# Rotary squares added on GpSimd, and projections and norms one step earlier, in a windowed-attention kernel

## The chip, the cores and the metric

The kernel runs on one core of a Trainium2 chip. A core has five engines that run their own instruction streams: TensorE (PE, matrix multiplication; its weight loads are listed as PEld), VectorE (DVE), ScalarE (ACT), GpSimd (POOL) and SyncE (SP, which here only starts DMAs). They meet at semaphores. TensorE writes its results to PSUM[...]; VectorE and ScalarE read PSUM, GpSimd works on SBUF alone in this kernel. The metric is the device time of one execution in microseconds.

## The reference, cut to what matters

The input x has 2048 tokens of 128 features. The reference applies a six-layer local-attention transformer, then a linear-attention block, and then the six layers again with the same weights:

```python
x = x + 0.5 * _L0_ffn_ref(_layernorm(x), ...)     # six layers
x = x + _L0_attn_ref(_layernorm(x), ...)          # linear attention and an MLP
x = x + 0.5 * _L0_ffn_ref(_layernorm(x), ...)     # six layers again

# one of the six layers; 16 heads of 64, window 32
q, k, v = split(shift_tokens(x) @ Wqkv)
q = l2norm(q) * q_scale;  k = l2norm(k) * k_scale
q = q * cos * scale + rotate_half(q) * sin * scale
k = k * cos / scale + rotate_half(k) * sin / scale
sim = 8 * q @ k.T                                  # each 32-token window sees itself and the one before
x = softmax(masked sim) @ v @ Wo + x
x = gated_gelu_ffn(layernorm(shift_tokens(x))) + x # hidden width 341
```

The change concerns `l2norm`: the sum of squares of a head's 64 query or key features. The kernel holds the features of a head as two rotary halves of 32, so that a sum of squares has two parts.

## The kernel before, in words

Data are kept transposed, features on partitions and tokens along the row: xa is the stream between layers, xf the stream between attention and feed-forward. All arithmetic is fp32 except the mask.

`ffn_module(m, last)` runs the six layers; it is called twice, and `linear_module` stands between the calls. A layer is cut into NAC = 8 chunks c of AC = 256 tokens, and the feed-forward into NCH = 4 pieces f of CH = 512 tokens. The attention of a chunk has four steps, each for 128 tokens and half of the heads.

The parts that the change touches, for layer l and chunk c:

- `tables(l, s)` (L187): four GpSimd products that scale the rotary tables for queries (s = 0) or keys (s = 1), once a layer.
- `project(l, c, g)` (L203), g = 0 to 3: for queries and for keys two matmuls (L218) write the two halves of four heads into one PSUM bank each. `rotate(s)` (L222) multiplies the bank by the tables on VectorE (prod, L224) and adds the two products on GpSimd into abq or abk (L230). `square(s)` (L234) takes the bank's squares on ScalarE into a tile sq (L236) of 128 x 2 x 256: half, token. There are four sq tiles, two abq tiles and three abk tiles in turn.
- `square_sums(l, c, g2)` (L247): matmuls with 32 columns of a selection matrix sum the squares over the partitions of each head into the PSUM tile ss. Four column groups u take four sq tiles; the two halves are added by accumulation, so there are eight matmuls a call and two calls a chunk (L254).
- `norms_a` (L310) and `norms_b` (L321): a reciprocal square root with one Newton step. VectorE clamps ss (L314), ScalarE takes logarithm, exponential and square (L315, L316, L318), VectorE finishes rn in two instructions (L325, L326).
- `scale_keys(l, c, g2)` (L342): two matmuls r (L347) spread rn over the partitions, two VectorE products scale abk with it (L353), and `gather` (L293) then starts eight DMAs that bring the keys into head order, hk. `gather(l, c, "q", g2)` does the same for unscaled queries, hq; query norms go into the softmax's scale through `query_norms` (L328: matmuls nt, copy rq).

Around them stand `values_proj` (pv, L271, copied to v by ScalarE, L272), `values_windows` (three DMAs that lay out windows, ve and vo), `earlier_keys` (pk, L367), `similarities` (sim, L383 and L391, then maxima and their scaling on VectorE, L402 and L403), `exponentials` (eight of L417 a step on ScalarE), `normalised` (reciprocal L427, product on GpSimd L429), `transposed` (te, L443, copied to eT by VectorE, L444), `values` (av, L458, copied to oT by ScalarE, L464), `output` (y, L471, xf, L475) and `feed_forward` (a generator; mean, variance, broadcast, then three gates: matmuls pf (L513), a table load, the gelu gate (L518) and a table load back on ScalarE, then the product h (L522) on VectorE, and the output yf (L530, L534)).

The order of all this is written out by hand. `at(step, pos, fn, ...)` puts a call into a plan, and the plan is emitted by step and, in a step, by position; every engine then executes its instructions in that order. Step t0 = 32 l + 4 c is the first of chunk c's four steps of similarities, so each step holds a projection of a later chunk, the similarities of this one and the values of an earlier step. With four steps a chunk and eight a feed-forward piece the plan repeats every eight steps. Nothing but semaphores on data and on reused buffers holds the engines together. The PSUM tiles called small share five banks in turn, ss has one and sim has two; which earlier tile a new one replaces follows from the order of the calls.

The lines of the plan that the change touches, before it:

```python
at(t0 - 7 + g, 20, project, l, c, g)
at(t0 - 6 + 2 * g2, 45, square_sums, l, c, g2)
at(t0 - 3, 2, norms_a, l, c)
at(t0 - 3, 33, norms_b, l, c)
at(t0 - 3, 58, scale_keys, l, c, 0)
at(t0 - 2, 45, scale_keys, l, c, 1)
```

Of the kernel before, what the change touches and what calls it, by code (L numbers as in the profile page):

```python
# [10 lines left out]
ALU = mybir.AluOpType  # L11
# [29 lines left out]
def kernel(ctx: ExitStack, tc: tile.TileContext, a: dict, out: bass.AP):  # L41
    nc = tc.nc
# [19 lines left out]
    sel = const.tile([P, 3, 32], F32, name="sel")  # L62
# [63 lines left out]
    def ffn_module(m, last):  # L126
        with ExitStack() as st:
            wp = st.enter_context(tc.tile_pool(name=f"w{m}", bufs=1))

            def load_qk(l, g):  # L130
                w = wp.tile([P, 4, P], F32, tag=f"wqk{g}", name=f"wqk{g}_{m}_{l}")
                nc.sync.dma_start(w, a["Wqk"][l].rearrange("p (g f) -> p g f", g=4)[:, g, :]
                                  .rearrange("p (u f) -> p u f", u=4))
                return w
# [47 lines left out]
            def small(name):  # L182
                return ps_small.tile([P, CH], F32, tag="small", name=name)
# [14 lines left out]
            def chunk(l, c):  # L198
                if (l, c) not in chunks:
                    chunks[l, c] = {"nm": f"{m}_{l}_{c}"}  # L200
                return chunks[l, c]

            def project(l, c, g):  # L203

                d = chunk(l, c)
                nm = f"{d['nm']}_{g}"
                if g % 2 == 0:
                    for qk, bufs in (("q", 2), ("k", 3)):
                        d[qk, g // 2] = work.tile(
                            [P, 2, 2, AC], F32, tag=f"ab{qk}", name=f"ab{qk}_{nm}", bufs=bufs  # L210
                        )
                xs = xa[:, c * AC : (c + 1) * AC]
                both = []
                for s in range(2):
                    ps = small(f"p{s}_{nm}")
                    both.append(ps.rearrange("p (u t) -> p u t", u=2))
                    for u in range(2):
                        nc.tensor.matmul(  # L218
                            both[s][:, u, :], wqk[g][:, 2 * s + u, :], xs, start=True, stop=True
                        )  # L220

                def rotate(s):  # L222
                    prod = work.tile([P, 2, 2, AC], F32, tag="prod", name=f"prod{s}_{nm}", bufs=2)
                    nc.vector.tensor_tensor(  # L224
                        prod,
                        both[s].unsqueeze(2).to_broadcast([P, 2, 2, AC]),
                        tabs[l, s].rearrange("p (u v) t -> p u v t", u=2),
                        ALU.mult,
                    )
                    nc.gpsimd.tensor_tensor(  # L230
                        d["qk"[s], g // 2][:, :, g % 2, :], prod[:, 0], prod[:, 1], ALU.add
                    )

                def square(s):  # L234
                    sq = work.tile([P, 2, AC], F32, tag="sq", name=f"sq{s}_{nm}", bufs=4)
                    nc.scalar.activation(sq, both[s], AF.Square)  # L236
                    d["sq", g, s] = sq


                rotate(0)  # L240
                square(1)
                square(0)
                rotate(1)
                if c == NAC - 1 and l + 1 < DEPTH:
                    wqk[g] = load_qk(l + 1, g)

            def square_sums(l, c, g2):  # L247

                d = chunk(l, c)
                if g2 == 0:  # L250
                    d["ss"] = ps_ss.tile([P, 2, AC], F32, tag="ss", name=f"ss_{d['nm']}")
                for half in range(2):
                    for u in range(4):
                        nc.tensor.matmul(  # L254
                            d["ss"][32 * u : 32 * u + 32, 0, :],
                            sel[:, g2, :],
                            d["sq", 2 * g2 + u % 2, u // 2][:, half, :],
                            start=(g2 == 0 and half == 0), stop=(g2 == 1 and half == 1),
                        )

            def values_proj(l, c, i):

# [289 lines left out]
            def at(step, pos, fn, *args):  # L552
                plan.setdefault(step, []).append((pos, len(plan[step]) if step in plan else 0, fn, args))
# [5 lines left out]
            for l in range(DEPTH):  # L559
                for c in range(NAC):  # L560

                    t0 = per * l + STEPS * c
                    if c == 0:
                        at(t0 - 10, 46, tables, l, 0)
                        at(t0 - 8, 46, tables, l, 1)
                    for g in range(4):
                        at(t0 - 7 + g, 20, project, l, c, g)
                        at(t0 - 2 + g, 50, values_proj, l, c, g)
                    for g2 in range(2):
                        at(t0 - 6 + 2 * g2, 45, square_sums, l, c, g2)  # L570
                    for t in range(2):
                        at(t0 - 1 + 2 * t, 62, values_windows, l, c, t)
                    at(t0 - 5, 30, gather, l, c, "q", 0)
                    at(t0 - 3, 1, gather, l, c, "q", 1)
                    at(t0 - 3, 2, norms_a, l, c)
                    at(t0 - 3, 33, norms_b, l, c)
                    at(t0 - 3, 58, scale_keys, l, c, 0)
                    at(t0 - 2, 45, scale_keys, l, c, 1)
                    at(t0 - 2, 46, query_norms, l, c)
                    at(t0 - 1, 45, earlier_keys, l, c)  # L580
                    for s in range(STEPS):
                        at(t0 + s, 25, similarities, l, c, s)
                        at(t0 + s, 30, exponentials, l, c, s, 0)
                        at(t0 + s, 51, exponentials, l, c, s, 1)
                        at(t0 + s + 1, 3, normalised, l, c, s)
                        at(t0 + s + 2, 40, transposed, l, c, s, 0)
                        at(t0 + s + 2, 41, transposed, l, c, s, 1)
                        at(t0 + s + 2, 60, values, l, c, s)
                    for t in range(2):
                        at(t0 + 4 + 2 * t, 55, output, l, c, t)  # L590
                for f in range(NCH):
                    gen = feed_forward(l, f)
                    t0 = per * l + 8 * f
                    for step, pos in (
                        (11, 57), (12, 57), (13, 4), (13, 57),
                        (15, 57), (17, 57), (19, 57), (21, 57),
                    ):
                        at(t0 + step, pos, more, gen)
# [112 lines left out]
    def no_earlier():  # L711

        nc.gpsimd.memset(xa[64:P, 0:1], 0.0)

    ffn_module(0, False)
    linear_module()
    no_earlier()
    ffn_module(1, True)


# [103 lines left out]
```

## Time and profile before

| what | value |
|---|---|
| runs | 4289.59 us median of 3 (4288.85 to 4295.82) |
| the profiled execution | 4295.45 us, of which its span is 4293.6 us |
| granted TensorE clock, mean | 0.959 |
| squares, L236, ACT | 768 of 0.60 us, 435.6 us |
| sums of squares, L254, PE | 3072 records, 249.1 us |
| rotary adds, L230, POOL | 768 of 1.27 us, 974.7 us |
| norms on ACT, L315, L316, L318 | 96 each of 0.40, 0.37 and 0.38 us |
| norms on DVE, L314, L325, L326 | 96 each of 0.43, 0.41 and 0.42 us |
| key scaling, L353, DVE | 384 of 0.68 us |

An fp32 matmul appears as two records, so that 3072 records of L254 are 1536 matmuls. Matmuls are pipelined and the ends of their records are modelled: two records that follow each other overlap in the list, and the difference of their starts says what one costs. "[1.88 <-ACT gate L518]" behind an instruction says that its engine had been idle for 1.88 us before it, until line 518 on ACT released it. In a table of stages the clock's column is the granted share of TensorE's full clock.

### The profile page before, as it was taken

The numbers are of one execution on the slowest core, as the hardware profiler recorded it, in microseconds if no ns is written. First come the engines' busy times: TensorE is split into PE (matmuls) and PEld (weight loads), VectorE is DVE, ScalarE is ACT, GpSimd is POOL, SyncE is SP. The second block draws the span as 40 slices with busy tenths as digits, with TensorE's granted clock in tenths as the row PEclk, the third lists the DMA queues.
The fourth block names the chain that finished last, engine by engine and source line by source line (L and its number), as shares of the span: only waits on it lengthen the run. The fifth ranks groups of instructions, "written<-read, shape, count | busy, mean of one in ns | idle before, by whom it ended". The sixth has DMA issues, their size and how long they took to land.

```text
span 4293.6 us, 110203 instructions
## 1 busy us (share of the span) xinstructions
PE 3947.0 (92%) x41968; PEld 2744.5 (64%) x41968; DVE 2719.7 (63%) x5222; ACT 2846.8 (66%) x8784; POOL 1672.7 (39%) x1355
## 2 busy tenths in 40 slices
PE   7899999999999999999777899999999999999998
PEld 4666666666666666666445666666666666666665
DVE  4666666666676666665426566666666666766664
ACT  4676777767667676677225676767667676677766
POOL 4343444344344334332014344343343443443331
PEclk8999999999999999999788999999999999999998
DMA  3343433433334334342003343433434334343331
GB/s 105 86 107 89 101 100 94 103 94 101 97 92 112 93 95 110 87 102 68 8 25 91 85 109 89 104 98 96 101 95 107 93 96 106 87 109 97 91 99 49
DMA packets 323975, 393.67 MB, mean 92 GB/s; under 512 B 61052, under 2 KB 274808, under 8 KB 323448
## 3 DMA queue, kind: packets, MB, share of 16 engines
q1 hardware_dynamic: 323448, 386.61, 35.7%
q8 instruction: 334, 5.47, 0.5%
q14 instruction: 193, 1.58, 0.1%
HBM read 34.58 MB, written 1.05 MB: 8 GB/s over the span
## 4 chain that ended last, share of the span: by engine, by line
PE 23%; ACT 16%; DVE 7%; issue 2%; SPq 1%; DMA 1%; POOL 1%; ACTq 0%; DVEq 0%; POOLq 0%
ACT e L417 8%; PE p L218 5%; DVE prod L224 3%; PE y L471 2%; PE te L443 2%; ACT L516 2%; PE pv L271 2%; PE av L458 2%; PE sim L391 2%; PE ss L254 2%; SPq L305 1%; ACT v L272 1%; DVE sim L402 1%; ACT gate L518 1%; PE yf L530 1%
## 5 line engine op out<-in xcount | busy, mean ns | idle before, releaser
L417 ACT ACTIVATE e<-sim,st,rq 128x96 f32<-128x96 f32 x3072 | 1291.8, 440 | 570.9 <-DVE st L403 509.5
L429 POOL TENSOR_TENSOR e<-e,st 128x768 f32<-128x768 f32 x384 | 564.4, 1470 | 1869.1 <-DVE st L427 1540.3
L224 DVE TENSOR_TENSOR prod<-p,tab 128x1024 f32<-128x1024 f32 x768 | 918.6, 1211 | 235.5 <-ACT sq L236 129.4
L218 PE MATMUL p<-xa,wqk 128*128 128x256 f32 x3072 | 845.0, 420 | 120.4 <-ACT gate L518 115.4
L218 PEld LDWEIGHTS p<-xa,wqk 128*128 128x128 f32 x3072 | 592.0, 204 | 246.6 <-ACT gate L518 138.1
L236 ACT ACTIVATE sq<-p 128x512 f32<-128x512 f32 x768 | 435.6, 599 | 355.6 <-PE p L218 240.0
L417 ACT ACTIVATION_READ_ACCUMULATOR e<-sim,st,rq 128x1 f32 x3072 | 653.9, 213 | 0.0
L230 POOL TENSOR_TENSOR abq<-prod 128x512 f32<-128x512 f32 x384 | 489.0, 1273 | 188.2 <-DVE prod L224 144.4
L230 POOL TENSOR_TENSOR abk<-prod 128x512 f32<-128x512 f32 x384 | 485.7, 1265 | 72.5 <-DVE prod L224 63.7
L444 DVE COPY eT<-te 96x512 f32<-96x512 f32 x768 | 489.8, 677 | 3.6 <-PE te L443 3.6
L522 DVE SCALAR_TENSOR_TENSOR h<-pf,lvec,gate 128x512 f32<-128x512 f32 x144 | 107.9, 749 | 571.1 <-ACT gate L518 553.1
L471 PEld LDWEIGHTS y<-oT,wo 128*128 128x128 f32 x3072 | 374.4, 192 | 95.1 <-issue 49.5
L402 DVE TENSOR_REDUCE sim<-sim 128x4 f32<-128x384 f32 x768 | 426.5, 555 | 9.0 <-PE sim L391 8.8
L443 PE MATMUL te<-sq_consts,e 128*96 128x128 f32 x3072 | 424.1, 279 | 2.5 <-ACT gate L518 0.8
L271 PE MATMUL pv<-wv,xa 128*128 128x512 f32 x768 | 415.4, 623 | 10.6 <-DVE rstd L499 8.4
L458 PE MATMUL av<-eT,ve 96*64 96x64 f32 x6144 | 406.9, 229 | 4.6 <-DVE eT L444 4.5
L458 PEld LDWEIGHTS av<-eT,ve 96*64 96x64 f32 x6144 | 318.3, 138 | 132.5 <-issue 50.5
L272 ACT COPY v<-pv 128x512 f32<-128x512 f32 x384 | 227.6, 593 | 255.3 <-DMA ve<-v 171.1
L458 PE MATMUL av<-eT,vo 96*64 96x64 f32 x6144 | 385.8, 223 | 0.0
L471 PE MATMUL y<-oT,wo 128*128 128x128 f32 x3072 | 376.4, 276 | 4.5 <-ACT gate L518 3.0
L391 PEld LDWEIGHTS sim<-hk,hq 64*64 64x64 f32 x12288 | 279.1, 136 | 151.7 <-issue 136.4
L443 PEld LDWEIGHTS te<-sq_consts,e 128*96 128x96 f32 x3072 | 317.6, 127 | 59.5 <-DVE h L522 11.8
(141 smaller groups left out, 4954.9 us busy)
## 6 DMA issues: line engine op xcount, KB each, us to landing
hq<-abq SPq DMA_DIRECT2D x1536, 64.0 KB, 2.1
hk<-abk SPq DMA_DIRECT2D x1536, 64.0 KB, 2.1
vo<-v SPq DMA_DIRECT2D x192, 384.0 KB, 4.3
ve<-v SPq DMA_DIRECT2D x192, 256.0 KB, 3.5
ve<-v SPq DMA_DIRECT2D x180, 128.0 KB, 2.3
wqk<-in_Wqk SPq DMA_DIRECT2D x48, 256.0 KB, 3.6
wv<-in_Wv SPq DMA_DIRECT2D x24, 256.0 KB, 2.8
wo<-in_Wo SPq DMA_DIRECT2D x12, 512.0 KB, 5.0
```

The lines of the kernel that those rows point to most:

```text
L218: nc.tensor.matmul(both[s][:, u, :], wqk[g][:, 2 * s + u, :], xs, start=True, stop=True)
L224: nc.vector.tensor_tensor(prod, both[s].unsqueeze(2).to_broadcast([P, 2, 2, AC]), tabs[l, s].rearrange("p (u v) t -> p u v t", u=2), ALU.mult,
L230: nc.gpsimd.tensor_tensor(d["qk"[s], g // 2][:, :, g % 2, :], prod[:, 0], prod[:, 1], ALU.add)
L236: nc.scalar.activation(sq, both[s], AF.Square)
L271: nc.tensor.matmul(ps, xa[:, ti * P : (ti + 1) * P], wv[j], start=True, stop=True)
L402: nc.vector.tensor_reduce(peaks[par], sims[par], AX.X, ALU.max, negate=True)
L417: nc.scalar.activation(e[:, par, i, :], d["sims", step][par][:, i, :], AF.Exp, bias=st8[:, 0, par, i : i + 1], scale=rq[:, par, i : i + 1] ...
L429: nc.gpsimd.tensor_tensor(ef, ef, st8[:, 1].rearrange("p r i -> p (r i)").unsqueeze(2).to_broadcast([P, 8, SK]), ALU.mult,)
L443: nc.tensor.transpose(te3[0:SK, i, :], d["e", step][:, par, i, :], ident)
L444: nc.vector.tensor_copy(d["eT", step][:, 4 * par : 4 * par + 4, :], te3[0:SK])
L458: nc.tensor.matmul(av3[64 * par : 64 * par + 64, i, SQ * s : SQ * s + SQ], d["vs", t][s][:, h * DH : (h + 1) * DH], d["eT", step][:, 4 * p ...
L471: nc.tensor.matmul(y[:, 0:P], wo[:, i, :], d["oT", t][:, i, :], start=(i == 0), stop=(i == 7))
```

## The change

Each pair of squared halves is added in place on GpSimd after the projection's rotations, so that `square_sums` has one matmul per column group and call where it had two. In the plan, `tables`, `project`, `square_sums`, the second query gather and the norms stand one step earlier; `square_sums` moves from position 45 to 61, behind the values at 60, and `scale_keys` to position 27, behind the similarities at 25, in the steps t0 - 3 and t0 - 2 where it was.

```diff
                 def square(s):
                     sq = work.tile([P, 2, AC], F32, tag="sq", name=f"sq{s}_{nm}", bufs=4)
                     nc.scalar.activation(sq, both[s], AF.Square)
-                    d["sq", g, s] = sq
+                    d["sq", g, s] = sq[:, 0, :]
+                    return sq
 
 
                 rotate(0)
-                square(1)
-                square(0)
+                sqs = [square(1), square(0)]
                 rotate(1)
+                for sq in sqs:
+                    nc.gpsimd.tensor_tensor(sq[:, 0, :], sq[:, 0, :], sq[:, 1, :], ALU.add)
...
-                for half in range(2):
-                    for u in range(4):
-                        nc.tensor.matmul(
-                            d["ss"][32 * u : 32 * u + 32, 0, :],
-                            sel[:, g2, :],
-                            d["sq", 2 * g2 + u % 2, u // 2][:, half, :],
-                            start=(g2 == 0 and half == 0), stop=(g2 == 1 and half == 1),
-                        )
+                for u in range(4):
+                    nc.tensor.matmul(
+                        d["ss"][32 * u : 32 * u + 32, 0, :],
+                        sel[:, g2, :],
+                        d["sq", 2 * g2 + u % 2, u // 2],
+                        start=(g2 == 0), stop=(g2 == 1),
+                    )
...
                     if c == 0:
-                        at(t0 - 10, 46, tables, l, 0)
-                        at(t0 - 8, 46, tables, l, 1)
+                        at(t0 - 11, 46, tables, l, 0)
+                        at(t0 - 9, 46, tables, l, 1)
                     for g in range(4):
-                        at(t0 - 7 + g, 20, project, l, c, g)
+                        at(t0 - 8 + g, 20, project, l, c, g)
                         at(t0 - 2 + g, 50, values_proj, l, c, g)
                     for g2 in range(2):
-                        at(t0 - 6 + 2 * g2, 45, square_sums, l, c, g2)
+                        at(t0 - 7 + 2 * g2, 61, square_sums, l, c, g2)
...
                     at(t0 - 5, 30, gather, l, c, "q", 0)
-                    at(t0 - 3, 1, gather, l, c, "q", 1)
-                    at(t0 - 3, 2, norms_a, l, c)
-                    at(t0 - 3, 33, norms_b, l, c)
-                    at(t0 - 3, 58, scale_keys, l, c, 0)
-                    at(t0 - 2, 45, scale_keys, l, c, 1)
+                    at(t0 - 4, 1, gather, l, c, "q", 1)
+                    at(t0 - 4, 2, norms_a, l, c)
+                    at(t0 - 4, 33, norms_b, l, c)
+                    at(t0 - 3, 27, scale_keys, l, c, 0)
+                    at(t0 - 2, 27, scale_keys, l, c, 1)
```

## The prediction, made before the changed kernel had run

> **What bounds the kernel now.** I read the page's busy shares first, then busy time by stage, then the timelines of single engines inside one stage.
>
> ```profile
> PE 3947.0 (92%) x41968; PEld 2744.5 (64%) x41968; DVE 2719.7 (63%) x5222; ACT 2846.8 (66%) x8784; POOL 1672.7 (39%) x1355
> ```
>
> The 92% invites the reading "TensorE bound", but matmul records overlap. The stages say more. Take as time zero of a step the start of its projection (p, L218) on TensorE. Steps repeat every eight: call them 0 to 7, where 0 and 4 hold the first similarities of a chunk, 7, 1 and 3 the feed-forward's three gates, 3 its mean, 4 its variance, 5 its broadcast and output; outputs y fall in the even steps. Busy time of eight successive stretches, here steps 2, 3, 4, 5, 6, 7, 0, 1 (columns: stretch, length, PE, PEld, DVE, ACT, POOL busy, granted clock, DMA share, GB/s):
>
> ```profile
> 3211.48:3223.22 11.74, 11.74 (x125) 8.52 (x125) 8.77 (x17) 5.84 (x16) 3.92 (x3) 0.85 0.44 112
> 3223.22:3232.25 9.03, 9.03 (x97) 5.76 (x93) 5.11 (x9) 7.07 (x28) 3.92 (x3) 1.00 0.44 111
> 3232.25:3243.44 11.19, 10.33 (x128) 7.83 (x125) 7.43 (x15) 9.20 (x24) 3.97 (x3) 1.00 0.46 120
> 3243.44:3253.56 10.12, 10.12 (x106) 6.87 (x102) 7.55 (x17) 7.06 (x26) 3.95 (x3) 1.00 0.21 59
> 3253.56:3263.74 10.18, 10.18 (x129) 7.66 (x125) 8.39 (x17) 4.29 (x13) 4.69 (x4) 1.00 0.41 93
> 3263.74:3271.53 7.79, 7.79 (x93) 5.27 (x89) 5.02 (x9) 6.05 (x24) 4.18 (x4) 1.00 0.50 135
> 3271.53:3282.41 10.88, 9.83 (x119) 6.91 (x116) 6.56 (x13) 9.20 (x27) 4.91 (x4) 1.00 0.47 117
> 3282.41:3293.10 10.69, 8.51 (x96) 5.52 (x92) 5.96 (x13) 8.96 (x30) 4.00 (x3) 1.00 0.14 33
> ```
>
> Over the projections' starts in both modules eight steps take 82.3 us, 48 times: 3950 of the 4294. Steps 3, 5, 6, 7 are full on TensorE. Steps 4, 0 and 1 are not, and there ACT carries 9 us: it loads two tables of 1.28 us around each gate. One gate and what follows, ACT and DVE in step 0:
>
> ```profile
> 3274.57 1.28 ACT L521 ACT_TABLE_LOAD   x1
> 3275.87 0.58 ACT L464 COPY oT<-av 128x512 f32<-128x512 f32 x1
> 3276.35 1.09 ACT L236 ACTIVATE sq<-p 128x512 f32<-128x512 f32 x2
> ...
> 3277.05 1.22 DVE L224 TENSOR_TENSOR prod<-p,tab 128x1024 f32<-128x1024 f32 x1 [0.52 <-ACT sq L236]
> ...
> 3279.53 1.27 DVE L444 COPY eT<-te 96x512 f32<-96x512 f32 x2
> ```
>
> From the gate's end (3274.55) the chain runs table, oT, squares, second rotation, two maxima, eT (done 3280.80). The value matmuls av need eT; they start at 3281.33, only 0.53 us later. In step 4 that slack is 1.31 us (eT done 3241.05, av 3242.36). The last thing to see is TensorE's restart in step 2, and the clock just after it:
>
> ```profile
> 3211.48 2.54 PE L218 MATMUL p<-xa,wqk 128*128 128x256 f32 x8 [1.88 <-ACT gate L518]
> ...
> 3212.80:3216.20 3.40, 3.40 (x39) 2.10 (x38) 3.03 (x6) 1.70 (x3) 2.52 (x2) 0.50 0.21 54
> ```
>
> p waits 1.88 us for a PSUM bank that the gate holds; then the clock halves for one stretch and step 2 takes 11.7 us; in groups without it, 10.2. It happens in most groups.
>
> [...]
>
> **The change, part by part.**
> *Half of the sums.* A call of L254 at full clock takes 1.00 us to the next matmul's start for 16 records, of which about 0.15 is filling; 8 records take 0.57. 192 calls x 0.43 = 82 us of TensorE work gone, 1.7 per group.
>
> *Adds on GpSimd.* 768 adds of 256 elements. Lower bound half of L230, 0.64 us[...]; I take 0.68: 522 us more, POOL at 2195, 51%. In each step they follow the abk add, which in step 1 ends at +5.3 (3287.71 in the trace), so they end near +6.7; ss, now last in the step after av, starts at +8.9. Two microseconds of cover; without it ss would wait one for one, and with it the p queued behind it on TensorE.[...]
>
> *The move of ss* from steps 2, 6, 4, 0 (after te) to 1, 5, 3, 7 (after av). It no longer waits for squares just made (the waits list has 54.9 us of that), but lengthens those four steps by 0.57 each.
>
> *Lead of one step.* Projections' DMAs: hq's eight issues (0.64 each) go out in step 3 or 7 as before, though abq is now rewritten one step sooner: landed at about +10.5, wanted at about +13. The second hq set goes out in step 0, where SP is free. Key gathers leave in steps 1 and 2 right after the scaling, landing near step 2 +4.0 before abk is rewritten at +4.8. The windows' DMAs no longer queue behind them, so ACT's waits for v (171 us) go; they lay beside other work, since steps 2 and 6 are TensorE's. Nothing here. The two tables of a layer (four L191 of 0.92 us each) move by a step too, into POOL time that stays idle. Prologue and tail of each module shift by one step: +2 us each by the short steps of 2 to 7 us there.
>
> *Norms from steps 1, 5 to 0, 4.* On ACT this is L315, L316, L318:
>
> ```profile
> 3283.29 0.43 ACT L315 ACTIVATE ss<-ss 128x256 f32<-128x256 f32 x1
> 3283.75 0.37 ACT L316 ACTIVATE ss<-ss 128x256 f32<-128x256 f32 x1
> 3284.15 0.38 ACT L318 ACTIVATE rn<-ss 128x256 f32<-128x256 f32 x1
> ```
>
> They take 1.15 us from L315's start to the next squares', and they now stand behind the gate's table and oT and ahead of the squares, just in the steps after gates (7 to 0, 3 to 4). On DVE L325 and L326 (0.78 together) stand ahead of eT. So eT comes 1.15 + 0.78 = 1.93 later after the gate. Step 0: 1.93 - 0.53 slack = +1.4. Step 4: 1.93 - 1.31 = +0.6. What leaves steps 1 and 5 was hidden there by TensorE and the gate.
>
> *Key norms behind the similarities.* In the changed order each r takes its PSUM bank from a finished te, y or gate, and p in step 2 reuses the banks of te instead of the gate's: the 1.88 us wait at its front goes. But pv, yf or the gate's pf now reuse r's bank, which L353 frees only after rotations and maxima, at +6.0, while TensorE gets there at +5.2 to +5.5. Step 5: yf waits 0.74, plus ss 0.57: 10.12 becomes 11.4. Step 6: pv waits 0.88, less the 1.0 of ss: 10.18 becomes 10.0. Together +1.1. Steps 1 and 2: the chain decides. Gate done at +10.65 in step 1 as before, table and oT to +12.5, rotation, maxima, L353 to +16.3, then pv 0.96, y 1.88, av 1.08: 20.3, where the mean before was 22.4: -2.1, of which 1.5 is the mean cost of the slow clock.
>
> Sum per group against this one: +1.4 + 0.6 + 1.1 - 2.1 = +1.0. Carried from step to step the lengths of steps 1 to 7 and then 0 come to 9.5, 10.8, 9.6, 11.3, 11.4, 10.0, 8.8 and 11.4: 82.8 against the mean of 82.3, where steps 7 and 0 are somewhat longer than in the group shown. I take +0.5.
>
> *The slow clock.* It isn't gone. In step 0 TensorE now waits about 1.1 us ahead of y and 2.3 ahead of av: longer than the 1.88 of before, beside the light av. I assume the fall as often as before, about three groups in four, now on the p of step 1; it delays p by 0.7 to 1.5 us, and the rotation chain with it: +0.9 per group. Bounds: 0 (never falls) to +2.5 (also in step 2, where 1.4 us of waiting follows te and nt, and in step 4, where 1.5 follows var).
>
> Total: 48 x (0.5 + 0.9) + 4 = +71 us. The profiled execution has a span of 4293.6, 4295.45 with what lies around it; the median of the runs is 5.9 lower. 4289.6 + 71 = 4360 us.
>
> **Rivals.**
> *TensorE is the bound and norms stay hidden* (faster). For it: 92%, and four full steps. Against it: 0.53 us of slack at step 0. Fully hidden, steps 0 and 4 would lose ss and its waits (about 1.4 and 1.3) less 0.57 for the ss moved into 7 and 3; with -2.1 and +1.1 a group takes 79.3, 4150 us. It decides from eT: if eT's delay after the gate stays under 0.53 us in step 0 and 1.31 in step 4. Partly hidden it lies anywhere up to 4280; I put it at 4220.
> *The chain lengthens but the clock no longer falls:* 48 x 0.5 + 4 = +28, 4318. For it: the waits are spread over more places.
> *The clock falls twice in a group:* +2.5 instead of 0.9, 4437.
> *GpSimd becomes a bound:* at 5.4 of 10 us a step it can't, unless an add takes 1.7 us; included in the last.
>
> **How the numbers follow.** Forecast 0.45 (4360); no fall 0.20 (4318); norms hidden wholly or partly 0.25 (4220); two falls 0.10 (4437). The range 4225 to 4435 leaves out half of the hidden case's lower part and half of the last. 0.2% is 8.6 us, about what a measurement of this kernel can tell from no change: faster 0.24, same 0.07, slower 0.69. The forecast's own range is 4325 to 4400.
>
> **What would show it.** Right: L254 with half its records; POOL near 2190 us; eT in step 0 finishing about 8.2 us after the gate (6.3 before) and av waiting for it; L315 to L318 between oT and squares of that step; p of step 2 without a wait for the gate; PE waits for L353 ahead of pv and yf; a step 0 of 11.4 and a step 5 of 11.4. The low clock would stand in step 1. Wrong: groups under 82 us, with av in step 0 starting when y ends; or ss waiting for GpSimd.

## The result, and the profile after

The changed kernel takes 4464.73 us, median of 4 runs (4457.75 to 4474.2), against 4292.7 for the kernel before in the same comparison: a ratio of 1.0399, interval 1.0372 to 1.0426. It is slower, as forecast, but by 172 us and not by 71, and so outside the range. Its profiled execution has a span of 4463.7 us.

The page's busy shares of the changed kernel (columns: engine, busy us, share of the span, instructions):

```profile
PE 3905.2 (87%) x40432; PEld 2716.9 (61%) x40432; DVE 2750.8 (62%) x5222; ACT 2846.6 (64%) x8784; POOL 2203.1 (49%) x2123
```

TensorE does 42 us less in a span that is 170 us longer. GpSimd does 530 us more (522 forecast), ScalarE nothing new. Engines did not become busier; they wait.

Eight steps of the changed kernel, in the order 2, 3, 4, 5, 6, 7, 0, 1 and with the columns of the table before (stretch, length, busy time of the engines, granted clock, DMA share, GB/s):

```profile
2835.25:2845.99 10.74, 9.24 (x112) 7.23 (x108) 7.80 (x16) 7.64 (x23) 5.39 (x6) 1.00 0.51 125
2845.99:2855.59 9.60, 9.60 (x104) 5.99 (x100) 4.91 (x8) 6.53 (x22) 5.31 (x5) 1.00 0.36 89
2855.59:2866.75 11.16, 9.51 (x113) 7.32 (x109) 7.80 (x16) 9.36 (x27) 5.32 (x5) 1.00 0.49 119
2866.75:2878.89 12.14, 11.00 (x113) 7.04 (x111) 9.42 (x18) 6.71 (x26) 5.44 (x6) 1.00 0.11 29
2878.89:2889.14 10.25, 9.24 (x112) 7.23 (x108) 7.08 (x14) 5.23 (x20) 6.07 (x7) 1.00 0.67 168
2889.14:2897.88 8.74, 8.74 (x102) 5.75 (x98) 4.91 (x8) 5.69 (x21) 5.31 (x5) 1.00 0.37 91
2897.88:2909.83 11.95, 9.23 (x105) 7.02 (x101) 7.41 (x16) 9.90 (x28) 5.34 (x6) 0.95 0.47 117
2909.83:2920.90 11.07, 10.44 (x102) 6.56 (x102) 6.20 (x10) 6.94 (x22) 5.37 (x5) 0.90 0.08 20
```

Of the four full steps only 3 and 7 are left. Steps 0, 2, 4, 5 and 6 each have 1.0 to 2.7 us in which TensorE has nothing to do, and the low clock has moved to the seam of steps 0 and 1. Over steps 24 to 183 of both modules (20 groups each, without the pipeline's filling and its end) a group of eight takes 85.9 us, before 82.3. "Group" below is always this mean.

What makes step 0 long can be read engine by engine. ScalarE's timeline of the changed kernel (start, duration, instruction), behind the gate, which ends at 2900.04, and the table load of 1.28:

```profile
2901.35 0.58 ACT L465 COPY oT<-av 128x512 f32<-128x512 f32 x1
2901.83 0.38 ACT L316 ACTIVATE ss<-ss 128x256 f32<-128x256 f32 x1
...
2902.64 0.38 ACT L319 ACTIVATE rn<-ss 128x256 f32<-128x256 f32 x1
2902.92 1.08 ACT L236 ACTIVATE sq<-p 128x512 f32<-128x512 f32 x2
```

VectorE's timeline of the same step:

```profile
2903.61 1.23 DVE L224 TENSOR_TENSOR prod<-p,tab 128x1024 f32<-128x1024 f32 x1 [1.26 <-ACT sq L236]
...
2906.09 0.41 DVE L326 SCALAR_TENSOR_TENSOR rn<-rn,ss 128x256 f32<-128x256 f32 x1
...
2906.88 1.28 DVE L445 COPY eT<-te 96x512 f32<-96x512 f32 x2
```

And TensorE's, with the waits in brackets:

```profile
2904.05 2.05 PE L472 MATMUL y<-oT,wo 128*128 128x128 f32 x16 [0.94 <-ACT sq L236]
2907.61 0.33 PE L459 MATMUL av<-eT,ve 96*64 96x64 f32 x2 [1.51 <-DVE eT L445]
...
2909.83 3.04 PE L218 MATMUL p<-xa,wqk 128*128 128x256 f32 x8
```

The norms (L316 to L319, L326, L327) stand where the forecast put them. eT is done 8.12 us after the gate, 6.25 before. TensorE waits 0.94 us for the PSUM bank that the squares free (a bank is here one of the kernel's eight PSUM tiles of 128x512 values) and 1.51 for eT, and then the projection of step 1 takes 3.04 us instead of 1.99. The stretch around it, from the windows of the changed kernel, has the clock at 0.50:

```profile
2908.57:2911.98 3.41, 3.41 (x31) 2.93 (x28) 0.29 (x2) 1.52 (x7) 1.47 (x1) 0.50 0.00 0
```

Groups of the page that answer to the other parts of the change (busy, mean ns | idle before, releaser):

```profile
L245 POOL TENSOR_TENSOR sq<-sq 128x256 f32<-128x256 f32 x768 | 540.6, 724 | 0.0
L272 PE MATMUL pv<-wv,xa 128*128 128x512 f32 x768 | 421.0, 631 | 117.8 <-DVE abk L354 116.5
```

TensorE waits 116.5 us for the key norms' scaling in front of pv alone; the groups of yf and pf have another 41.8 and 25.6. The wait of p for the gate, 115.4 us before, is 9.2 now. One wait went, and a larger set came.

### The profile page after: what moved, and what is told of

Its sections match the earlier page's. It is cut to its first block, busy times and chain, and to the rows that moved or that the text cites. A ratio compares the mean times of both kernels' runs of the same rounds, so it can differ in the third digit from the quotient of the medians.

```text
span 4463.7 us, 108227 instructions
## 1 busy us (share of the span) xinstructions
PE 3905.2 (87%) x40432; PEld 2716.9 (61%) x40432; DVE 2750.8 (62%) x5222; ACT 2846.6 (64%) x8784; POOL 2203.1 (49%) x2123
## 4 chain that ended last, share of the span: by engine, by line
PE 19%; DVE 12%; ACT 11%; issue 3%; DMA 2%; POOL 2%; SPq 1%; DVEq 0%; POOLq 0%; ACTq 0%
PE p L218 5%; ACT e L418 5%; DVE prod L224 4%; PE av L459 3%; DVE sim L403 3%; PE y L472 2%; ACT sq L236 2%; DVE abk L354 2%; PE pv L272 2%; PE pf L514 1%; SPq L306 1%; PE yf L531 1%; DMA ve<-v 1%; POOL e L430 1%; ACT L517 1%
## 5 line engine op out<-in xcount | busy, mean ns | idle before, releaser
L224 DVE TENSOR_TENSOR prod<-p,tab 128x1024 f32<-128x1024 f32 x768 | 929.7, 1215 | 554.8 <-PE p L218 295.7
L236 ACT ACTIVATE sq<-p 128x512 f32<-128x512 f32 x768 | 422.1, 597 | 482.0 <-PE p L218 429.4
L459 PE MATMUL av<-eT,ve 96*64 96x64 f32 x6144 | 451.4, 234 | 142.8 <-DVE eT L445 98.6
L245 POOL TENSOR_TENSOR sq<-sq 128x256 f32<-128x256 f32 x768 | 540.6, 724 | 0.0
L459 PEld LDWEIGHTS av<-eT,ve 96*64 96x64 f32 x6144 | 356.8, 142 | 301.1 <-DVE eT L445 134.3
L272 PE MATMUL pv<-wv,xa 128*128 128x512 f32 x768 | 421.0, 631 | 117.8 <-DVE abk L354 116.5
L472 PEld LDWEIGHTS y<-oT,wo 128*128 128x128 f32 x3072 | 387.0, 201 | 197.3 <-ACT sq L236 139.3
L472 PE MATMUL y<-oT,wo 128*128 128x128 f32 x3072 | 405.5, 288 | 69.2 <-ACT sq L236 64.8
L459 PE MATMUL av<-eT,vo 96*64 96x64 f32 x6144 | 418.1, 229 | 0.0
L444 PE MATMUL te<-sq_consts,e 128*96 128x128 f32 x3072 | 414.5, 278 | 3.2 <-ACT sq L236 2.1
L465 ACT COPY oT<-av 128x512 f32<-128x512 f32 x384 | 224.6, 585 | 212.9 <-PE av L459 211.5
```

The lines of the kernel that those rows point to most:

```text
L224: nc.vector.tensor_tensor(prod, both[s].unsqueeze(2).to_broadcast([P, 2, 2, AC]), tabs[l, s].rearrange("p (u v) t -> p u v t", u=2), ALU.mult,
L245: nc.gpsimd.tensor_tensor(sq[:, 0, :], sq[:, 0, :], sq[:, 1, :], ALU.add)
L272: nc.tensor.matmul(ps, xa[:, ti * P : (ti + 1) * P], wv[j], start=True, stop=True)
L444: nc.tensor.transpose(te3[0:SK, i, :], d["e", step][:, par, i, :], ident)
L459: nc.tensor.matmul(av3[64 * par : 64 * par + 64, i, SQ * s : SQ * s + SQ], d["vs", t][s][:, h * DH : (h + 1) * DH], d["eT", step][:, 4 * p ...
L472: nc.tensor.matmul(y[:, 0:P], wo[:, i, :], d["oT", t][:, i, :], start=(i == 0), stop=(i == 7))
```

## The experiments

Times are medians; the kernel before measured 4291.7 to 4297.0 in these comparisons. Line numbers shift by a few from kernel to kernel, so tiles are named as well. "Filling" is the first 24 projection steps of a module, which begin with projections alone. "Low clock" is the total length of the stretches of one trace at half clock: 352 us before, 403 after; of these 137 and 181 lie in the 40 groups, the rest in the fillings, between the modules and at the ends. A "fall" is the beginning of such a stretch.

| kernel | us | ratio to before | group | filling (two modules) |
|---|---|---|---|---|
| before | 4292 | 1 | 82.3 | 210.7, 210.5 |
| changed | 4464.7 | 1.0399 [1.0372, 1.0426] | 85.9 | 216.6, 220.2 |
| e1 key norms back | 4411.8 | 1.0264 [1.0233, 1.0295] | 84.8 | 207.2, 211.2 |
| e2 halves back | 4426.6 | 1.0312 [1.0288, 1.0336] | 85.5 | 202.7, 203.4 |
| e8 sums run twice | 4464.1 | 1.0399 [1.0381, 1.0418] | 85.9 | 220.4, 221.0 |
| e3 before + additions, late sums | 4297.6 | 1.0005 [0.9997, 1.0014] | 82.0 | 220.8, 220.9 |
| e11 before + late sums | 4333.1 | 1.0078 [1.0058, 1.0098] | 83.0 | 215.2, 215.5 |
| e4 norms behind squares and eT | 4309.6 | 1.0038 [1.0023, 1.0053] | 82.3 | 221.1, 221.7 |
| e5 = e4 + e1 | 4203.2 | 0.9788 [0.9767, 0.9809] | 79.7 | 213.9, 214.4 |
| e6 = e5 + e2 | 4187.7 | 0.9758 [0.9740, 0.9776] | 80.2 | 192.3, 194.4 |
| e9 = e5, e2 while filling | 4165.0 | 0.9694 [0.9674, 0.9714] | 79.7 | 193.2, 193.8 |
| e7 before + ScalarE's norms twice, VectorE's moved | 4306.2 | 1.0029 [1.0020, 1.0038] | 82.2 | 218.0, 220.7 |
| e10 = e5, ScalarE's norms early | 4287.5 | 0.9972 [0.9962, 0.9982] | 81.9 | 205.7, 207.9 |
| e12 changed + one filler | 4441.3 | 1.0350 [1.0336, 1.0364] | 85.4 | 218.6, 218.2 |

The theory to begin with (A): the waits made the loss, through norms ahead of squares and eT, and key norms that hold banks. Rivals: (B) GpSimd's additions cost it; (C) the projections' lead does.

**e1: the key norms back** in their old positions.

```diff
-                    at(t0 - 3, 27, scale_keys, l, c, 0)
-                    at(t0 - 2, 27, scale_keys, l, c, 1)
+                    at(t0 - 3, 58, scale_keys, l, c, 0)
+                    at(t0 - 2, 45, scale_keys, l, c, 1)
```

> The changed kernel with scale_keys back at positions 58 and 45. Theory A (the loss is made of waits: the norms ahead of the squares and of eT in steps 0 and 4, the key norms' r banks ahead of pv, yf and pf in steps 1, 2, 5 and 6, and the slow clock that follows such waits): the 185 us in which TensorE waited for L354 before pv, yf and pf go, part of the gate's wait at p comes back; 4370 to 4420. Theory B (GpSimd's adds are what costs): nothing changes, 4455 to 4475. Theory C (the lead of the projections itself costs, through reused buffers): 4455 to 4475.

4411.8, 53 us less than the changed kernel, and 1.1 us less a group. A's size was right, but 119 of the 172 us remain.

**e2: no additions on GpSimd, two half sums on TensorE** (the diff's first two parts undone, the plan as changed).

> The changed kernel without the adds on GpSimd: both halves are summed by the matmuls again, the plan stays. Theory A: the sums stand at the ends of steps 1, 3, 5 and 7 where TensorE is on the path, so four times 0.43 us a group come back: 4465 + 48 x 1.7 = 4545, less some 50 us of waits for the adds that go: 4490 to 4550. Theory B: the loss goes, 4300 to 4350. Theory C: 4500 to 4550, as A.

4426.6, 38 us *less*. Halving TensorE's sums did not gain 82 us; the exchange costs 38. None of the three expectations had this. Two readings were open: the additions delay something, or the longer sums keep TensorE's clock up (the low-clock total fell from 403 to 291 us). The next run tells them apart.

**e8: additions kept, and the sums' matmuls run a second time** into the unused half of their bank.

```diff
-                for u in range(4):
-                    nc.tensor.matmul(
-                        d["ss"][32 * u : 32 * u + 32, 0, :],
+                for half in ((1, 0), (0, 1))[g2]:
+                    for u in range(4):
+                        nc.tensor.matmul(
+                            d["ss"][32 * u : 32 * u + 32, half, :],
...
```

> The changed kernel with its additions on GpSimd kept, and the sums' matmuls run a second time into the unused half of their bank, so that TensorE does as much as before. If GpSimd's additions are what the halves' undoing saved, this is no faster than the changed kernel, and up to 82 slower: 4460 to 4545. If the added TensorE work keeps the clock up, it is near the run with the halves undone although the additions are still there: 4415 to 4445, with a low-clock total near 290 us.

4464.1: the same as the changed kernel to 0.6 us, with twice the sums. The clock reading falls for this place: the low-clock total went down too, to 373, and nothing was gained. So TensorE's 1.7 us a group in the halved sums are worth nothing in the changed kernel, and e2's 38 us are the additions' delay. The steps show how: in e8 steps 3, 5 and 7 are 0.43 longer and steps 0, 2 and 4 0.4 to 0.6 shorter (medians), which fits even steps that end when the other engines' chain does. By the table, 31 of the 38 lie in the two fillings (216.6 + 220.2 against 202.7 + 203.4); what is left is within the spread of e2's own runs, 4418 to 4444. The changed kernel's groups of the sums, in a window behind the filling and in one that holds the first filling, show the same (the last column is TensorE's wait):

```profile
L255 PE MATMUL ss<-sq,sel 128*32 128x256 f32 x640 | 51.1, 391 | 0.0
```

```profile
L255 PE MATMUL ss<-sq,sel 128*32 128x256 f32 x112 | 15.1, 474 | 25.7 <-POOL sq L245 25.7
```

From 300 to 2020 us no sum waits for GpSimd. From 28 to 300 they wait 25.7 us.

**e3: the kernel before with the additions, and the halved sums at position 61 of their old steps,** no lead, norms and key norms as before.

> The kernel before with the adds on GpSimd alone: half of the sum matmuls, square_sums at position 61 of its old steps so that it stands behind the adds; no lead, norms and key norms as before. Theory A: 82 us of matmuls and the waits for squares go and no wait comes: 4150 to 4230. Theory B: about as slow as the changed kernel, above 4400. Theory C: as A.

4297.6, no difference from before: a miss for all three. **e11** takes the additions away again and leaves only the move of the sums.

```diff
-                        at(t0 - 6 + 2 * g2, 45, square_sums, l, c, g2)
+                        at(t0 - 6 + 2 * g2, 61, square_sums, l, c, g2)
```

> The kernel before with its sums of squares at the end of the step, both halves, no additions: a step beside the run that had the additions too (4298, eight steps 82.0). If the halved sums were worth TensorE's 1.7 us in eight steps there and the late sums cost them again, this is at 4360 to 4380. If TensorE has slack where the sums stand, so that halving them gains nothing, it is at 4260 to 4300, and below the run with additions by what these cost while the pipeline fills (about 20).

4333.1, between the two expectations. The late sums by themselves cost 0.6 us a group and 4.5 to 5 in each filling; the halving gives back 1.0 of its 1.7 a group; and the additions cost another 5.5 us in each filling. Three terms that nearly cancel made e3 look like nothing.

**e4: the changed kernel, with the norms split:** ScalarE's part behind the squares of the step's projection (position 22), VectorE's two behind the copies eT (43).

```diff
-                    at(t0 - 4, 33, norms_b, l, c)
+                    at(t0 - 4, 22, norms_s, l, c)
+                    at(t0 - 4, 43, norms_b, l, c)
...
```

> The changed kernel with the norms' three ScalarE instructions moved from position 2 (ahead of the squares) to 22 (behind the squares, in the gap of about 1.6 us in which ScalarE waits for the maxima) and norms_b from 33 to 43, behind eT. Theory A: eT in steps 0 and 4 comes 1.9 us earlier, at most 1.4 and 0.6 us of which reach the path, with part of the slow clock in step 1: 4465 - 48 x 2 to 3 = 4320 to 4370. Theories B and C: norms were never on the path, 4450 to 4470.

4309.6, 155 us less than the changed kernel, more than A had: step 0 goes from 11.7 to 9.6 and step 4 from 11.2 to 9.3 (medians). What remains against e5 is the key norms' wait. TensorE's timeline of e4 in step 2 shows it plainly (abk L359 there is L354 of the changed kernel):

```profile
2924.45 1.60 PE L272 MATMUL pv<-wv,xa 128*128 128x512 f32 x2 [1.51 <-DVE abk L359]
2925.84 3.16 PE L477 MATMUL y<-oT,wo 128*128 128x128 f32 x16
```

pv waits 1.51 us, and behind the wait pv and y take 1.60 and 3.16 us instead of 1.12 and 1.95. That was read as a fall, as in a step 2 of the changed kernel: there y takes 3.26 us behind a wait of pv of 1.49, and the stretch over it has the clock at 0.50:

```profile
1478.39:1481.80 3.41, 3.41 (x26) 3.19 (x27) 0.97 (x4) 2.06 (x9) 0.00 (x0) 0.50 0.37 92
```

**e5: e4 with the key norms back as in e1.**

> The changed kernel with the norms' ScalarE part in the gap behind the first squares (as in the run before) and with the key norms back behind the exponentials. If both losses are waits and add up, it takes the -155 of the norms and the -53 of the key norms: 4245 to 4275, below the kernel before by 20 to 45. If the lead of the projections costs something by itself, or the two undo the same wait, it stays at 4295 to 4320.

4203.2, faster than the kernel before by 2.1% and 42 us below the lower end of what was expected if both losses are waits. The key norms alone account for 106 us here (e4 against e5), where it was 53 beside the early norms: step 2 has a median of 10.2 instead of 12.2, step 5 10.8 instead of 12.9. C falls: with the norms out of the way the lead is a gain. e3 and e5 differ in the lead and the norms' place alone, and e5 is 94 us faster, 2.3 a group.

**e6: e5 without the additions,** two half sums.

> The same without GpSimd's additions, two half sums on TensorE. If the halved sums pay once the waits are out of the way, this is slower than the run with them by 40 to 80. If the additions' delay of the sums costs more than TensorE saves (what the changed kernel showed when its halves were undone, -38), it is faster by 20 to 40. If TensorE has slack and GpSimd too, within 10 of it.

4187.7, another 15.5 less, which is between two of the expectations. The group, though, is 0.5 *longer* (80.2 against 79.7). So e5's halved sums save it 20 us in 40 groups, and its additions cost it 42 in the two fillings; the two profiled spans differ by 20.4. TensorE's timeline of e5 in the first filling:

```profile
57.07 1.08 PE L255 MATMUL ss<-sq,sel 128*32 128x256 f32 x6 [3.18 <-POOL sq L245]
58.08 5.54 PE L218 MATMUL p<-xa,wqk 128*128 128x256 f32 x16
```

And of e6, the same call and the same next projections:

```profile
48.35 1.06 PE L254 MATMUL ss<-sq,sel 128*32 128x256 f32 x14 [1.52 <-ACT sq L236]
49.34 3.72 PE L218 MATMUL p<-xa,wqk 128*128 128x256 f32 x16
```

At the start of a filling a step is little but a projection, each with 2.5 us of rotation additions and 1.4 of the new ones on GpSimd. The sums wait for them, and the next projections stand behind the sums on TensorE.

**e9: e5 with e2's two half sums, and no additions, only for the first two chunks of a module.**

```diff
+            def filling(l, c):
+                return l == 0 and c < 2
...
-                for sq in sqs:
+                for sq in [] if filling(l, c) else sqs:
...
+                n = 2 if filling(l, c) else 1
```

> The run with norms in the gap, old key norms and GpSimd's additions (4203), but with the two half sums on TensorE again, and no additions, for the first two chunks of the first layer of each module, where the pipeline fills. In the two runs that differ by the additions alone, the first 24 steps of a module took 214 us with them and 193 without, and eight later steps 79.7 with and 80.2 without. If that is all, this has the 193 and the 79.7: 41 us below 4203, 4155 to 4170, the fastest of all. If the additions cost in every layer (a wait of TensorE that moves rather than goes), it stays within 10 of 4203.

4165.0, as worked out beforehand: filling of e6 (193), groups of e5 (79.7). It beats the kernel before by 3.1% and the changed one by 6.7%. ScalarE's timeline of e9 in step 0, from the end of the table load on, to set beside that of the changed kernel:

```profile
2941.02 0.58 ACT L475 COPY oT<-av 128x512 f32<-128x512 f32 x1
2941.50 1.21 ACT L239 ACTIVATE sq<-p 128x512 f32<-128x512 f32 x2
2942.61 0.38 ACT L326 ACTIVATE ss<-ss 128x256 f32<-128x256 f32 x1
```

And VectorE's:

```profile
2944.68 1.27 DVE L455 COPY eT<-te 96x512 f32<-96x512 f32 x2
```

eT is done 6.24 us after the gate's end (2939.71), which is the time before the change, and the step takes 9.5 us.

**e7: the kernel before with the norms split,** meant as a control for e4.

> The kernel before with only the norms' ScalarE part moved behind its first squares, no lead, no additions. If norms ahead of squares cost only where a gate, its table and an output copy lie ahead of them too (steps 0 and 4), there is little to gain here, where they stand in steps 1 and 5: 4270 to 4295. If norms ahead of squares cost anywhere, it gains some 1.2 us in each of two steps of eight: 4180 to 4240.

4306.2: 0.3% slower, all of it in the filling. But the kernel is not the control that was meant. Its early norms on ScalarE stayed in place, and a second set was added behind the squares; only VectorE's two instructions moved. Two groups of its list, of the early and of the late set:

```profile
L315 ACT ACTIVATE ss<-ss 128x256 f32<-128x256 f32 x96 | 38.5, 401 | 0.8 <-DVE ss L314 0.7
L325 ACT ACTIVATE ss<-ss 128x256 f32<-128x256 f32 x96 | 36.8, 384 | 0.2
```

So it can't say what taking the norms away from the front of steps 1 and 5 is worth. It shows that a second set of 1.1 us on ScalarE, with VectorE's part later, leaves a group of the old plan as it was (82.2 against 82.3), and costs 17.5 us in the two fillings. What the norms' place does in the old plan stays open. The lead is better read from e11 and e6, both with late sums, two halves and old key norms: 4333.1 to 4187.7, and 83.0 to 80.2 a group, for the lead and the norms' new place together.

**e10: e5 with ScalarE's part of the norms early again,** VectorE's part still behind eT.

> The run with old key norms (projections and norms led by one more step), with the norms' ScalarE part ahead of the squares as the change has it, and only VectorE's part of 0.9 us moved behind the copies of the exponentials. 4412 is the time with both parts early, 4203 with both late. If each part delays its own engine's work one after the other, VectorE's share of the two us in steps 0 and 4 comes back: some 80 to 90, 4315 to 4335. If ScalarE's part alone sets it (squares late, so the bank of the output's matmuls and all behind it), it stays at 4395 to 4415. If VectorE's part alone sets it, 4200 to 4230.

4287.5. ScalarE's part costs 84 us (against e5), VectorE's 124 more (e1 against this run): neither alone sets it, and VectorE's share is over what was expected. By steps: ScalarE's part lengthens steps 0 and 4 by 1.08 each, close to its 1.15 us. VectorE's lengthens them by 0.8 and 1.0, and step 5 by 1.1 (medians 11.85 and 10.79), though nothing of it stands in step 5. TensorE's projection in one such step 5, of e1:

```profile
2997.31 3.03 PE L218 MATMUL p<-xa,wqk 128*128 128x256 f32 x8
```

And of e10:

```profile
2914.74 1.99 PE L218 MATMUL p<-xa,wqk 128*128 128x256 f32 x8
```

It is the clock again. In e1 a stretch of low clock lies over the seam of steps 4 and 5, from 2996.02 on (the mean granted clock is 0.81 from 2994.00 to 2997.30 and 0.64 from 2997.31 to 3000.30), behind this wait ahead of av, which e10 does not have:

```profile
2995.36 0.58 PE L459 MATMUL av<-eT,ve 96*64 96x64 f32 x3 [1.00 <-ACT v L273]
```

The price of such a wait is not fixed. The changed kernel has the same wait of 1.0 in all its steps 4, but a fall begins there in 5 of 40 groups, where e1 has 24; in the changed kernel 26 begin in step 0, in e1 6.

**e12: the changed kernel plus one matmul of 128x512 (a filler) in steps 0 and 4,** written to the bank of av ahead of the value matmuls that overwrite it.

```diff
+                if step == 2:
+                    nc.tensor.matmul(av, mean_w, xo[:, 0:CH], start=True, stop=True)
```

> The changed kernel with one more matmul of 128x512 of about 1.0 us on TensorE in steps 0 and 4, 96 in all, put ahead of the value matmuls where TensorE waits 1.5 and 1.0 us for eT; what it computes is overwritten. If those waits are what the clock falls on, the projections of steps 1 and 5 run at full clock (2.0 us instead of a mean of 2.8 and 2.2 in steps 1 and 5): the kernel does more and takes 25 to 50 less, 4415 to 4440, with a low-clock total of 320 to 360 instead of 403 us. If the clock follows the load or something else, the time stays at 4460 to 4475 and the low-clock total near 400; if the added matmul doesn't fit into the wait, it is up to 50 above.

4441.3: more work, and 23 us less, at the edge of what was expected for a clock that follows the waits. Low clock is at 298 us instead of 403, lower than expected. TensorE's timeline of e12 at the seam of steps 0 and 1:

```profile
3149.19 1.02 PE L456 MATMUL av<-xo,mean_w 128*128 128x512 f32 x2
3150.86 0.33 PE L461 MATMUL av<-eT,ve 96*64 96x64 f32 x2 [0.65 <-DVE eT L445]
...
3152.53 1.99 PE L218 MATMUL p<-xa,wqk 128*128 128x256 f32 x8
```

The projections of steps 1 and 5 take 1.99 us in all 40 groups (means of 2.83 and 2.22 in the changed kernel). In step 0 the filler stands in the wait for eT and leaves 0.65 of 1.51 us. In step 4 it does not. There the trace puts the wait of 1.0 us down to the copy v and not to eT, and the filler itself waits for it:

```profile
3106.62 1.12 PE L456 MATMUL av<-xo,mean_w 128*128 128x512 f32 x2 [1.00 <-ACT v L273]
```

So the wait stays in step 4, with a full matmul behind it, and the falls there go all the same. Step 1 is 0.8 us shorter and step 5 0.5; step 4 is 0.6 longer. And of the falls some only move: in steps 2 and 6, which have waits and no filler, falls begin in 16 and 12 groups of 40, in the changed kernel in 9 and 7.

## Why the prediction was right in direction and wrong in size

**What was right.** eT was put at about 8.2 us after the gate and is done at 8.12, and the norms stand between oT and the squares. An addition was taken at 0.68 us and GpSimd's busy time at 2195; measured are 0.724 and 2203. p in step 2 no longer waits for the gate. TensorE waits for L353, now L354, ahead of pv and yf. The clock falls on p of step 1, which was to cost 0.9 a group (p's mean is 2.83 instead of 1.99: 0.84). The lengths without a fall are close too. As means of the six groups of 40 that have none, steps 1 to 7 and 0 take 9.8, 10.7, 9.6, 11.2, 12.1, 10.3, 8.5 and 11.5, together 83.7; worked out were 9.5, 10.8, 9.6, 11.3, 11.4, 10.0, 8.8 and 11.4, together 82.8.

**The step that failed first: the slow clock.** The forecast let it fall in one place, for +0.9. The group of 85.9 less the 83.7 makes 2.2. Above their undisturbed lengths the means of step 1 have 0.8, step 2 0.4, step 6 and step 0 0.3 each, step 5 0.2, step 4 0.1; the last 0.1 is in step 7, which has no fall. Step 2 and step 4 had been named as places for "two falls", at a tenth; the mistake was to charge each fall only to the one wait that caused most of them before, although the sum itself placed waits of 0.7 to 2.3 us in five steps. In step 0 they were even shorter than worked out (0.94 and 1.51 us measured, 1.1 and 2.3 forecast). The falls that were not forecast are about 1.2 us a group, nearly 60 us over 48 groups. e12 shows that the falls of steps 0 and 4 hang on how much TensorE has to do just there: with one matmul of about 1 us more in each, the projections behind them take 1.99 us in all 40 groups, against means of 2.83 and 2.22. Why a given wait has a fall in one group and none in the next was not found.

**The second: when the key norms free their bank.** L353 was taken to end at +6.0 in step 5. TensorE's timeline of the changed kernel there:

```profile
2873.57 2.84 PE L531 MATMUL yf<-h,w 128*128 128x512 f32 x6 [1.14 <-DVE abk L354]
```

VectorE's has the reason:

```profile
2868.01 0.16 DVE L496 SCALAR_TENSOR_TENSOR rstd<-var,rstd 128x4 f32<-128x4 f32 x1 [0.81 <-ACT rstd L495]
...
2872.82 1.28 DVE L354 TENSOR_TENSOR abk<-abk,r 128x512 f32<-128x512 f32 x2 [0.24 <-issue]
```

In step 5 the feed-forward's rstd stands ahead of the rotation on VectorE and waits 0.81 us for ScalarE, so the first scaling ends at about +6.7 and yf starts at +6.82. (In step 6, which has no rstd, pv starts at +6.33: the +6.0 was a little short there too.) The step takes 12.1 instead of 11.4. With 0.3 each in steps 1 and 6, less 0.4 in others, the chain is 0.9 us a group over the forecast, about 42 us. Clock and chain together, with the filling counted like other groups, come to about the 105 us between 4360 and 4465.

**Norms, +1.4 in step 0 and +0.6 in step 4,** were reckoned from the steps as they were before, and the lengths that came of it were right: 11.4 and 11.3 worked out, 11.5 and 11.2 measured. What the main line didn't say is what the norms cost in the *new* plan. e1 against e5 is 208.6 us and 5.1 a group: 1.9 in step 0, 2.1 in step 4, and 1.1 by the clock in step 5. The slacks of 0.53 and 1.31 us that the forecast took off were slack of steps in which sums stood ahead of av. The same change moved these away, so that TensorE would have been through steps 0 and 4 in 9.5 and 9.4 us (e5), 1.2 and 1.8 less than before. The norms cost more than all of it.

**The halved sums** were right as TensorE time (a call takes 0.57 us to the next matmul) and were not simply credited as time; e8 puts their worth in the changed kernel at nothing, e5 against e6 at 0.5 us a group where the waits are gone. **The additions' cover of 2 us** held in every full step and failed in the filling, which the forecast priced at +2 us a module for the plan's shift alone: they cost 14 and 17 us there in the changed kernel (against e2), 21 a module in e5 (against e6). They did not slow VectorE: its rotations (L224) have a mean of 1215 ns after and 1211 before.

**The rival "norms hidden"** was given as 79.3 us a group and 4150 us; its parts, as they are written, sum to 79.7 and about 4170. It is not what the change did. e9 hides the norms and has 79.7 and 4165, but with other key norms and other sums in the filling, so that the nearness is in part luck. Still, the gain was there to be had. With the norms alone moved (e4) the changed kernel is at the time of the kernel before, 0.4% over it; with the key norms alone moved (e1) it is 2.6% over it; with both (e5) 2.1% under it. The order of a few instructions decided which side of zero the change fell on.

Where each part ended, going from before to after: lead, late sums and the norms' place behind squares and eT, together -104 (e6), then one thing at a time: additions with halved sums +15.5 (e5), norms early in the new plan +208.6 (e1), key norms early +53 (changed). That sums to +173, against 172 measured. In the first step the late sums alone are +36 in the old plan (e11); what the norms' place has in it was not measured. That the key norms' cost comes through r's bank was read from the waits and is as worked out, but no kernel with a bank of its own for r was run.

## What to carry to other kernels

When a plan moves a producer earlier, look at the first instruction behind it in the queue of every engine it uses, not only at when its result is wanted: 1.9 us of norms that nobody needed yet stood ahead of squares and eT that TensorE was about to wait for, and cost 209 us beside the old key norms (e1 against e5) and 155 beside the new (e4). Count a wait of TensorE in this kernel twice, once as idle time and once as the chance that the matmuls behind it run at half clock: in the changed kernel a stretch at 0.50 begins in step 0, where TensorE waits 0.94 and 1.51 us in the group shown, in 26 of 40 groups. And read the filling of a pipeline apart from its steady state: GpSimd is busy for 49% of the changed kernel's span, and the sums wait 25.7 us for it from 28 to 300 us and not at all from 300 to 2020.

## What the runs showed of the hardware that was not expected

Waits of 0.94 and 1.51 us with 2.05 us of y between them were followed, in the step 0 shown, by a stretch of 3.41 us at a clock of 0.50 over the seam of steps 0 and 1; such a stretch begins in one of these two steps in 28 of 40 groups. In the changed kernel's step 2 that begins at 1470.23, the 3.41 us at 0.50 followed a single wait of 1.49 us behind the small matmuls te and nt (1.08 and 0.61 us). Waits below 2 us were not safe here.

One useless matmul of about 1 us in the wait of step 0 and behind that of step 4 took 106 us off the low-clock total (85 of them in the 40 groups) and 23 us off the kernel. By contrast, running the sums twice (e8), at the ends of the odd steps where TensorE was at work anyway, lowered the total by 31 us and gained nothing: between these two kernels it counted where the work stood.
